# Second attention of a four-layer graph network: the threshold search's one-column chains moved from VectorE to GpSimd and rewritten

## The chip, the core and the metric

The kernel runs on one core of a Trainium2 chip. The metric is device time in microseconds (us) of one execution. Four compute engines work side by side, each through its own queue strictly in order: TensorE (PE in the profile, its weight loads PEld), VectorE (DVE), ScalarE (ACT) and GpSimd (POOL). SyncE (SP) starts the DMAs here. An instruction whose input comes from another engine waits at the head of its queue on a semaphore, and all that is queued behind it on that engine waits too. Measurements of this kernel agree within about 0.2%.

## The reference

Four graph layers work one after another on 3327 nodes with 256 features; each ends in `x = layernorm(x + layer(x, adj))`. The change touches the second of the two attention steps of the last layer:

```python
def _top_p_attention(X, W1, W2, W3):
    q = X @ W1.T @ W2.T
    k = X @ W3.T
    probs = softmax(q @ k.T / TAU)             # 3327 x 3327
    idx = argsort(-probs); sp = probs in that order; cs = cumsum(sp)
    keep_sorted = cs - sp < TOP_P              # TOP_P = 0.9
    A = probs * mask                           # the largest that hold 90% of the mass
    return A / max(A.sum(-1), 1e-12)

R = row-normalized (S + I); Xf = Xa = X; Z = 0
for n in range(2):
    A = _top_p_attention(Xa, W1, W2, W3)
    Xf = R @ Xf
    Xa = A @ Xa
    Z = Z + Xf @ U1[n].T + Xa @ U2[n].T
h = X + Z
return (h - mean) / sqrt(var + eps) * ln_g + ln_b
```

The hard part is the mask: for each row, the probability at which the sorted mass passes 0.9. The kernel doesn't sort; it searches for the threshold.

## The kernel before, in words

Rows are padded to 26 tiles of 128; a row of scores `e` is 128x3328 per tile and is cut in two halves of 1664 columns. The second attention is the last stage, from about 2650 us to the end of the span at 3517.5 us. One trip of its outer loop works on four tiles at once, at different steps, and the steps are interleaved by hand: generators are advanced by `next(...)` in a fixed sequence (`search(i)`, `slot(...)`, `next(result)`), and `here = tc.keep_in_program_order` pins the large instructions of PE and ACT to it. DVE and POOL instructions that are not pinned are ordered by the framework's scheduler. One trip holds:

- **Scores** (`scores`, L1038 on PE, copied to `e` by ACT in L1022): four chunks of the row for the tile two ahead. GpSimd fills one padding column (L1029).
- **Search** (`search_long`), which is what the change rewrites. (a) ACT makes two exponentials of the row: L1169 with half the exponent, whose row sum is `root`, and L1171, whose row sum is `total`. From these a first threshold `c1 = 0.301 (total/root)^2` is made on DVE (L1176 to L1182), and `lim = -0.9 total` on POOL (L1174). (b) ACT measures the row at `c1` with a Relu (L1184, sum `f1`) and a Sign (L1186, sum `sg`); from the count and mass above it, DVE makes a second threshold `c2` in one chain of one-column instructions (L1188 to L1204), while POOL makes the side values `big`, `s` and `ends` (L1207 to L1214). (c) ACT measures again at `c2` (L1216 Relu, L1218 Sign), and DVE makes the third threshold `c3` (L1220 to L1230). (d) DVE takes what lies below `c3` in both halves (`z`, L1236: a scalar_tensor_tensor whose two tensor inputs are both the row in SBUF), finds the eight largest of each 128 columns (13 MAX8 a half, L1103), ranks them (L1114, L1116), finds the crossing (L1123 to L1126), works out ties (L1251 to L1260), drops ties (two match_replace, L1266), and masks the whole row in place (L1274, a scalar_tensor_tensor with both inputs in SBUF, 128x3328).
- **Diffusion** (`diffused`): POOL makes `t` (L1068, L1072), PE sums 26 products (L1058), DVE adds (L1077).
- **Attention values** (`attended`): PE transposes the masked row four blocks at a time (`tp`, L1087), ACT copies each group out of PSUM (`wt`, L1089 through the wrapper in L1022), PE multiplies (L1091). Groups of copies lie in ACT's pinned order between the search's seven row-wide instructions.
- **Result** (`second`): DVE adds (L1318) and takes statistics (L88, L89). POOL adds the bias (L1320), makes `1/sqrt(var)` (`power`: L821 an add, L822 a power, both 128x1), normalizes (L1326 a tensor_scalar, L1327 and L1328 tensor_tensors, all 128x256), and after a second pair of statistics again L821, L822 and L1336. ACT writes the final normalization (L1337).

A chain step for one tile is one instruction on 128x1: one number per row. So the search consists of a few large instructions, and between them DVE and POOL chains whose cost is not data but instruction time.

Two lines order things explicitly: `bound[0]` is the last instruction of chain (b), and each match_replace is issued behind the newest one (`with tc.issue_after(bound[0].ins)`).

Of the kernel before, what the change touches and what calls it, by code (L numbers as in the profile page):

```python
# [9 lines left out]
F32 = mybir.dt.float32  # L10
# [3 lines left out]
ALU = mybir.AluOpType  # L14
# [33 lines left out]
def gnn_kernel(ctx: ExitStack, tc: tile.TileContext, n: int, a: dict, out: bass.AP):  # L48
# [763 lines left out]
    with tc.tile_pool(name="l3", bufs=1) as pool, tc.tile_pool(name="l3d", bufs=1, space=DRAM) as dram:  # L812
# [184 lines left out]
        sd = dram.tile([nt, P, D], F32, name="sd")  # L997
        u1, u2 = (load(pool, x) for x in ("U1", "U2"))
        g3, b3 = (load_row(pool, x) for x in ("ln3_g", "ln3_b"))
        factors = pool.tile([P, 4], F32, name="factors")  # L1000
        for k, x in enumerate((-0.5, -1.0, 0.3, 1.5)):
            nc.vector.memset(factors[:, k:k + 1], x)
        ones = pool.tile([P, 8 * max(RP0, RPT)], F32, name="ones")
        nc.vector.memset(ones, 1.0)
# [144 lines left out]
            yield  # L1149

        junks = [None]
        bound = [None]

        def search_long(work, sm, e, total, v, kept, halves=False):

            def t(name):  # L1160
                return t1(sm, name)

            m8, neg, root = t1(sm, "m8", 8), t1(sm, "neg", 2), t("root")
            nc.vector.max(m8, e[:, :KC])
            nc.gpsimd.tensor_scalar(neg, factors[:, :2], m8[:, 0:1], None, op0=ALU.mult)

            junk = junks[0] = junks[0] or work.tile([P, npad], BF16, name="junk", bufs=1)
            yield
            here(nc.scalar.activation(junk, e, AF.Exp, bias=neg[:, 0:1], scale=0.5, accum_out=root))  # L1169
            yield  # L1170
            here(nc.scalar.activation(e, e, AF.Exp, bias=neg[:, 1:2], accum_out=total))  # L1171
            yield
            lim = t("lim")
            nc.gpsimd.tensor_scalar(lim, total, -TOP_P, None, op0=ALU.mult)  # L1174
            c1 = t("c1")
            nc.vector.reciprocal(c1, root)  # L1176
            nc.vector.tensor_mul(c1, c1, total)
            nc.vector.scalar_tensor_tensor(c1, c1, 0.301, c1, op0=ALU.mult, op1=ALU.mult)


            nc1, f1, sg, k1, m1 = t("nc1"), t("fs1"), t("sg"), t("k1"), t("m1")
            nc.vector.tensor_scalar_mul(nc1, c1, -1.0)  # L1182
            yield
            here(nc.scalar.activation(junk, e, AF.Relu, bias=nc1, accum_out=f1))  # L1184
            yield
            here(nc.scalar.activation(junk, e, AF.Sign, bias=c1, scale=-1.0, accum_out=sg))  # L1186
            yield
            nc.vector.tensor_scalar(k1, sg, -0.5, npad / 2, op0=ALU.mult, op1=ALU.add)  # L1188
            nc.vector.scalar_tensor_tensor(m1, k1, c1, f1, op0=ALU.mult, op1=ALU.add)
            rc, na = t("rc"), t("na")  # L1190
            nc.vector.reciprocal(rc, c1)
            nc.vector.tensor_scalar(na, m1, lim, rc, op0=ALU.add, op1=ALU.mult)

            den, nu, p, q = t("den"), t("nu"), t("p"), t("q")
            nc.vector.tensor_scalar(den, k1, 0.5, UNDER, op0=ALU.mult, op1=ALU.add)
            nc.vector.reciprocal(den, den)
            nc.vector.tensor_scalar(nu, na, UNDER, den, op0=ALU.add, op1=ALU.mult)
            nc.vector.tensor_scalar(p, nu, 0.0, 1.0, op0=ALU.max, op1=ALU.add)
            nc.vector.tensor_sub(q, p, nu)
            nc.vector.reciprocal(q, q)  # L1200
            c2 = t("c2")
            nc.vector.scalar_tensor_tensor(c2, p, c1, q, op0=ALU.mult, op1=ALU.mult)
            nc2, f2, k2, m2 = t("nc2"), t("fs2"), t("k2"), t("m2")
            bound[0] = nc.vector.tensor_scalar_mul(nc2, c2, -1.0)  # L1204

            big = t("big")
            nc.gpsimd.tensor_tensor(big, k1, na, op=ALU.subtract)  # L1207
            nc.gpsimd.tensor_scalar(big, big, 32.0, HUGE, op0=ALU.is_lt, op1=ALU.mult)

            s, dm, ends, same = t("s"), t("dm"), t1(sm, "ends", 2), t("same")  # L1210
            nc.gpsimd.tensor_tensor(s, c2, c1, op=ALU.subtract)
            nc.gpsimd.tensor_scalar(same, s, 0.0, None, op0=ALU.is_equal)
            nc.gpsimd.tensor_tensor(s, s, same, op=ALU.add)
            nc.gpsimd.tensor_scalar(ends, factors[:, 2:], k1, 1.0, op0=ALU.mult, op1=ALU.max)  # L1214
            yield
            here(nc.scalar.activation(junk, e, AF.Relu, bias=nc2, accum_out=f2))  # L1216
            yield
            here(nc.scalar.activation(junk, e, AF.Sign, bias=c2, scale=-1.0, accum_out=sg))  # L1218
            yield
            nc.vector.tensor_scalar(k2, sg, -0.5, npad / 2, op0=ALU.mult, op1=ALU.add)  # L1220
            nc.vector.scalar_tensor_tensor(m2, k2, c2, f2, op0=ALU.mult, op1=ALU.add)
            nc.vector.reciprocal(s, s)
            nc.vector.tensor_sub(dm, m1, m2)
            nc.vector.tensor_mul(s, s, dm)
            nc.vector.tensor_scalar(s, s, ends[:, 0:1], ends[:, 1:2], op0=ALU.max, op1=ALU.min)
            nc.vector.reciprocal(s, s)
            c3 = t("c3")
            nc.vector.scalar_tensor_tensor(c3, c2, UNDER, m2, op0=ALU.mult, op1=ALU.add)
            nc.vector.tensor_scalar(c3, c3, lim, s, op0=ALU.add, op1=ALU.mult)
            nc.vector.scalar_tensor_tensor(c3, c3, c2, big, op0=ALU.add, op1=ALU.max)  # L1230
            rest, base = t("rest"), t("base")
            cand = candidates(work)
            for h, r in enumerate((rest, base)):
                part = e[:, h * half:(h + 1) * half]
                z = work.tile([P, half], F32, name="z", bufs=1)
                x = nc.vector.scalar_tensor_tensor(z, part, c3, part, op0=ALU.is_lt, op1=ALU.mult, accum_out=r)  # L1236
                if h:
                    here(x)
                yield
                segment_tops(cand[:, h * half // SEG * 8:], z, half // SEG)  # L1240
                yield

            nc.gpsimd.tensor_scalar(base, base, rest, total, op0=ALU.add, op1=ALU.subtract)
            nc.gpsimd.tensor_scalar(rest, big, 1.0, base, op0=ALU.is_lt, op1=ALU.mult)
            base = rest
            top = ranked(work, cand, RPT)
            cs = crossing(work, v, top, base, lim, ALU.subtract, ALU.is_le)
            yield
# [12 lines left out]
            sums = t1(sm, "sums", 2)  # L1261
            for i, c in enumerate((0, half)):
                drop = drops[:, i, :]
                part = e[:, c:c + half]
                with tc.issue_after(bound[0].ins):
                    nc.vector.match_replace(part[:, ::-1], drop, part[:, ::-1], 0.0)  # L1266
                if halves:
                    nc.vector.scalar_tensor_tensor(part, part, v, part, op0=ALU.is_ge, op1=ALU.mult,
                                                   accum_out=sums[:, i:i + 1])
            yield  # L1270
            if halves:
                nc.vector.tensor_add(kept, sums[:, :1], sums[:, 1:])
            else:
                nc.vector.scalar_tensor_tensor(e, e, v, e, op0=ALU.is_ge, op1=ALU.mult, accum_out=kept)  # L1274
            yield
# [39 lines left out]
        def second(work, psum, it, acc, f, xf):  # L1315
# [5 lines left out]
            mv = small.tile([P, 2], F32, name="mv")  # L1321
            stats(mv, h)
            rs = small.tile([P, 1], F32, name="rs")
            power(rs, mv)
            yield
            nc.gpsimd.tensor_scalar(h, h, mv[:, 0:1], rs, op0=ALU.subtract, op1=ALU.mult)  # L1326
            nc.gpsimd.tensor_tensor(h, h, g3, op=ALU.mult)  # L1327
            nc.gpsimd.tensor_tensor(h, h, xb, op=ALU.add)  # L1328
            yield
# [40 lines left out]
        with tc.tile_pool(name="l3w", bufs=2) as work, tc.tile_pool(name="l3s", bufs=4) as sm, \  # L1370
# [41 lines left out]
            with tc.tile_pool(name="l3q", bufs=3, space=PSUM) as psum:  # L1412
                es, searches, xfs = {}, {}, []
                result = iter(())
                for i in range(-2, nt + 1):
# [52 lines left out]
                    if 0 < i:  # L1468
                        f = normalizer(sm, kepts[1][:, i - 1:i], tots[1][:, i - 1:i])
                        result = second(work, psum, i - 1, next(values), f, xfs[i - 1])  # L1470
                both(result)
                fl = unresolved(sm, psum, 1)

            fi0 = pool.tile([1, nt + 1], I32, name="fi0")
# [140 lines left out]
```

## Time and profile before

| what | value |
|---|---|
| median of 3 runs | 3516.83 us (3515.82 to 3521.38) |
| the profiled execution | 3519.38 us, its span 3517.5 us (1.9 us lie around it) |
| busy over the span | PE 92%, DVE 67%, ACT 49%, POOL 27% |
| second attention, 2750 to 3430 us (680 us) | PE 662.45, DVE 652.24, ACT 570.31, POOL 247.57 us busy |
| start of L1326, from 2876.58 to 3402.72 us | 17 trips, 30.95 us each |
| L1327 on POOL in that stage | 0.72 us at least, 2.25 us in the median |

How to read it: the shares over the span are averages over four layers with different limits, so only the rows of the second attention count here. A "group" is a set of instructions of one line, engine and shape with its count, its sum of busy time, the mean of one and the idle time just before. A timeline row has the start and the duration in us, the engine, the line, what is written from what, and in brackets the idle time before it with the instruction that ended it. PE's end times are modelled.

### The profile page before, as it was taken

What the parts mean: (1) busy time and instruction counts of PE and PEld (TensorE: products, weight loads), DVE (VectorE), ACT (ScalarE), POOL (GpSimd) and SP (SyncE); (2) the same over time, 40 slices, a digit from 0 to 9 for tenths busy, and PEclk for the clock granted to TensorE, in tenths of its full rate; (3) what the DMA queues carried; (4) which work ended last, traced back from release to release, by engine and by line L of the source; (5) the groups of instructions that cost most, each with busy time, mean ns of one, the idle gap of its engine ahead of it and who ended that gap; (6) DMA issues with size and microseconds to landing.
All of it is one profiled execution on the core that took longest, in us unless ns stands there. A gap on an engine that the chain in (4) does not pass through costs nothing. (4 is left out here: it accounts for less than half of the span.)

```text
span 3517.5 us, 43266 instructions
## 1 busy us (share of the span) xinstructions
PE 3235.5 (92%) x15597; PEld 2540.3 (72%) x15597; DVE 2370.4 (67%) x5245; ACT 1740.6 (49%) x2751; POOL 932.8 (27%) x942
## 2 busy tenths in 40 slices
PE   9999988988888766999899999999997999999996
PEld 7888766676676555888677878787775777777775
DVE  1111177999999997777454544444434999999996
ACT  0000356767667675111133333333336888888883
POOL 0000054666665653121100000000001243333332
PEclk9999998999999888999899999999999999999998
DMA  7443334334443222344321212121212112222220
GB/s 248 139 140 110 102 109 112 101 119 106 106 119 91 66 58 92 126 140 145 95 66 56 65 49 65 48 67 47 67 47 74 55 56 67 68 70 61 70 65 16
DMA packets 147577, 307.99 MB, mean 88 GB/s; under 512 B 19570, under 2 KB 68850, under 8 KB 147218
## 3 DMA queue, kind: packets, MB, share of 16 engines
q1 hardware_dynamic: 147346, 305.06, 29.7%
q8 instruction: 126, 2.06, 0.2%
q14 instruction: 105, 0.86, 0.1%
HBM read 294.36 MB, written 10.65 MB: 87 GB/s over the span
## 5 line engine op out<-in xcount | busy, mean ns | idle before, releaser
L274 POOL TENSOR_TENSOR h<-du,row 128x2048 f32<-128x2048 f32 (+1 forms) x110 | 465.7, 4233 | 339.3 <-DVE hc L274 270.8
L274 DVE TENSOR_TENSOR_SCAN h<-dA,carry,h 128x512 f32<-128x512 f32 (+1 forms) x384 | 448.7, 1220 | 19.8 <-ACT dA L281 19.7
L281 ACT ACTIVATE dA<-t,A_log 128x512 f32<-128x512 f32 (+1 forms) x448 | 292.3, 658 | 146.4 <-DVE h L274 143.4
L1058 PE MATMUL acc<-F,at 128*128 128x256 f32 x1352 | 353.5, 387 | 1.0 <-ACT q L832 0.6
L1091 PE MATMUL acc<-X,wt 128*128 128x256 f32 x1352 | 343.5, 390 | 10.5 <-ACT wt L1089 10.2
L1091 PE MATMUL acc<-G,wt 128*128 128x256 f32 x1352 | 336.8, 392 | 6.4 <-ACT wt L1022 5.9
L1091 PEld LDWEIGHTS acc<-X,wt 128*128 128x128 f32 x1352 | 242.6, 189 | 105.3 <-issue 41.3
L120 PE MATMUL acc<-xa,at 128*128 128x257 f32 x1352 | 308.6, 382 | 5.6 <-DMA at<-in_adjT 5.6
L1058 PE MATMUL acc<-X,at 128*128 128x256 f32 x1352 | 308.4, 381 | 0.0
L967 PE MATMUL acc<-F,at 128*128 128x257 f32 x1352 | 303.6, 381 | 1.2 <-DMA U<-in_U 1.2
L333 PE MATMUL cb<-F,at 128*128 128x256 f32 x1196 | 294.0, 394 | 7.4 <-ACT hn L353 4.5
L1091 PEld LDWEIGHTS acc<-G,wt 128*128 128x128 f32 x1352 | 250.1, 193 | 67.0 <-ACT wt L1022 36.8
L1103 DVE MAX8 cand<-e 128x8 f32<-128x128 f32 x676 | 142.2, 278 | 229.0 <-ACT e L1044 217.4
L1058 PEld LDWEIGHTS acc<-F,at 128*128 128x128 f32 x1352 | 237.9, 190 | 75.3 <-issue 50.2
L120 PEld LDWEIGHTS acc<-xa,at 128*128 128x128 f32 x1352 | 255.7, 191 | 42.4 <-issue 5.5
L1058 PEld LDWEIGHTS acc<-X,at 128*128 128x128 f32 x1352 | 252.9, 191 | 40.2 <-issue 7.0
L967 PEld LDWEIGHTS acc<-F,at 128*128 128x128 f32 x1352 | 253.4, 190 | 36.8 <-issue 1.4
L333 PEld LDWEIGHTS cb<-F,at 128*128 128x128 f32 x1196 | 228.8, 197 | 59.4 <-issue 14.3
L624 PE MATMUL y<-ident,hc 128*128 128x128 f32 x1664 | 229.7, 291 | 42.9 <-DVE hc L274 42.3
L624 PEld LDWEIGHTS y<-ident,hc 128*128 128x128 f32 x1664 | 204.5, 151 | 82.5 <-DVE hc L274 59.3
L274 DVE TENSOR_TENSOR hc<-h,row 128x2048 f32<-128x2048 f32 (+2 forms) x114 | 242.8, 2131 | 11.0 <-PE y L624 4.3
L1089 ACT COPY wt<-tp 128x512 f32<-128x512 f32 (+1 forms) x182 | 93.5, 557 | 309.2 <-PE tp L1087 309.0
(352 smaller groups left out, 5264.1 us busy)
## 6 DMA issues: line engine op xcount, KB each, us to landing
at<-in_adjT SPq DMA_DIRECT2D x102, 832.0 KB, 4.6
at<-in_adjT SPq DMA_DIRECT2D x260, 320.0 KB, 2.9
row<-bc SPq DMA_DIRECT2D x80, 512.0 KB, 5.1
at<-in_adjT SPq DMA_DIRECT2D x52, 576.0 KB, 4.0
at<-in_adjT SPq DMA_DIRECT2D x26, 512.0 KB, 3.8
row<-bc SPq DMA_DIRECT2D x32, 384.0 KB, 5.0
xt<-in_xT SPq DMA_DIRECT2D x26, 128.0 KB, 4.1
qd<-q SPq DMA_DIRECT2D x104, 32.0 KB, 1.9
```

Source lines behind the costliest of these rows:

```text
L120: nc.tensor.matmul(acc, at[:, j, :], rhs[:, j0 + j, :], start=(j0 + j == 0), stop=(j0 + j == nt - 1))
L274: return lambda *x, **k: tc.keep_in_program_order(op(*x, **k))
L281: decays.append(op(*x, **k))
L333: ten.matmul(acc, at[:, j % JC, :], X0[:, j, :], start=(j == 0), stop=(j == nt - 1))
L624: x = ten.matmul(y[:, g * P:(g + 1) * P], h[:, g, i * P:(i + 1) * P], ident, is_transpose=True, start=(first and g == 0), stop=(last and g ...
L967: nc.tensor.matmul(acc, at[:, j, :], F[:, j0 + j, :], start=(j0 + j == 0), stop=(j0 + j == nt - 1))
L1058: nc.tensor.matmul(acc, at[:, j, :], rhs[:, j0 + j, :], start=(j0 + j == 0), stop=(j0 + j == nt - 1))
L1089: copy(wt[:, :m, :], pt[:, :m, :])
L1091: nc.tensor.matmul(acc, wt[:, j, :], rhs[:, j0 + j, :], start=(j0 + j == 0), stop=(j0 + j == nt - 1))
L1103: nc.vector.max(cand[:, s * 8:(s + 1) * 8], z[:, s * SEG:(s + 1) * SEG])
```

## The change

Three things are changed, all in the second attention.

1. The chains that make `c1`, `c2` and `c3` are put on GpSimd as a whole. Reciprocals become powers with exponent -1, and two columns are worked at once where `c` and `-c` are wanted. `root^-2` and its products with 0.301 and -0.301 (`squares`) are made behind the first exponential, so that only one instruction (`c1s`) lies between `total` and the Relu at `c1`. The update of `c2` is written with fewer quotients.
2. The wait of match_replace on `bound` is dropped.
3. In `second`, the first `power` and the first normalization (the old L1326) are issued behind the newest `c3` instruction (`edge`), on GpSimd's queue.

```diff
-        factors = pool.tile([P, 4], F32, name="factors")
-        for k, x in enumerate((-0.5, -1.0, 0.3, 1.5)):
+        factors = pool.tile([P, 8], F32, name="factors")
+        for k, x in enumerate((-0.5, -1.0, 0.3, 1.5, 0.301, -0.301, -2.0, -1.0)):
...
-        bound = [None]
+        edge = [None]
+
+        def behind_edge():
+            return tc.issue_after(edge[0].ins) if edge[0] is not None else nullcontext()
...
             here(nc.scalar.activation(junk, e, AF.Exp, bias=neg[:, 0:1], scale=0.5, accum_out=root))
             yield
+            squares = t1(sm, "squares", 2)
+            nc.gpsimd.tensor_tensor(root, root, factors[:, 6:7], op=ALU.pow)
+            nc.gpsimd.tensor_scalar(squares, factors[:, 4:6], root, None, op0=ALU.mult)
             here(nc.scalar.activation(e, e, AF.Exp, bias=neg[:, 1:2], accum_out=total))
             yield
-            lim = t("lim")
-            nc.gpsimd.tensor_scalar(lim, total, -TOP_P, None, op0=ALU.mult)
-            c1 = t("c1")
-            nc.vector.reciprocal(c1, root)
-            nc.vector.tensor_mul(c1, c1, total)
-            nc.vector.scalar_tensor_tensor(c1, c1, 0.301, c1, op0=ALU.mult, op1=ALU.mult)
-            nc1, f1, sg, k1, m1 = t("nc1"), t("fs1"), t("sg"), t("k1"), t("m1")
-            nc.vector.tensor_scalar_mul(nc1, c1, -1.0)
+            gps = nc.gpsimd
+            def scaled(dst, x, a, b, op0, op1):
+                return gps.tensor_scalar(dst, x, a, b, op0=op0, op1=op1)
+            def raised(x, k):
+                gps.tensor_tensor(x, x, factors[:, k:k + 1], op=ALU.pow)
+            c1s, lim, rc = t1(sm, "c1", 2), t("lim"), t("rc")
+            scaled(c1s, squares, total, total, ALU.mult, ALU.mult)
+            c1, nc1 = c1s[:, 0:1], c1s[:, 1:2]
+            gps.tensor_scalar(lim, total, -TOP_P, None, op0=ALU.mult)
+            gps.tensor_tensor(rc, c1, factors[:, 7:8], op=ALU.pow)
...
             here(nc.scalar.activation(junk, e, AF.Sign, bias=c1, scale=-1.0, accum_out=sg))
             yield
-            nc.vector.tensor_scalar(k1, sg, -0.5, npad / 2, op0=ALU.mult, op1=ALU.add)
...
-            bound[0] = nc.vector.tensor_scalar_mul(nc2, c2, -1.0)
...
+            scaled(k1, sg, -0.5, npad / 2, ALU.mult, ALU.add)
+            scaled(m1, k1, c1, f1, ALU.mult, ALU.add)
+            na, more, room, less = t("na"), t("more"), t("room"), t("less")
+            scaled(na, m1, lim, rc, ALU.add, ALU.mult)
+            scaled(room, k1, 0.5, UNDER, ALU.mult, ALU.add)
+            scaled(more, na, UNDER, 0.0, ALU.add, ALU.max)
+            gps.tensor_tensor(more, more, room, op=ALU.add)
+            scaled(less, more, na, UNDER, ALU.subtract, ALU.subtract)
+            raised(less, 7)
+            c2, nc2, f2, k2, m2 = t("c2"), t("nc2"), t("fs2"), t("k2"), t("m2")
+            scaled(c2, more, less, c1, ALU.mult, ALU.mult)
+            gps.tensor_scalar(nc2, c2, -1.0, None, op0=ALU.mult)
+            yield
+            here(nc.scalar.activation(junk, e, AF.Relu, bias=nc2, accum_out=f2))
...
+            gps.tensor_tensor(s, c1, c2, op=ALU.subtract)
+            gps.tensor_scalar(same, s, 0.0, None, op0=ALU.is_equal)
+            gps.tensor_tensor(s, s, same, op=ALU.add)
+            raised(s, 7)
+            scaled(ends, factors[:, 2:4], k1, 1.0, ALU.mult, ALU.max)
             here(nc.scalar.activation(junk, e, AF.Sign, bias=c2, scale=-1.0, accum_out=sg))
             yield
-            nc.vector.tensor_scalar(k2, sg, -0.5, npad / 2, op0=ALU.mult, op1=ALU.add)
...
-            nc.vector.scalar_tensor_tensor(c3, c3, c2, big, op0=ALU.add, op1=ALU.max)
+            scaled(k2, sg, -0.5, npad / 2, ALU.mult, ALU.add)
+            scaled(m2, k2, c2, f2, ALU.mult, ALU.add)
+            scaled(s, m2, m1, s, ALU.subtract, ALU.mult)
+            scaled(s, s, ends[:, 0:1], ends[:, 1:2], ALU.max, ALU.min)
+            raised(s, 7)
+            c3 = t("c3")
+            scaled(c3, c2, UNDER, m2, ALU.mult, ALU.add)
+            scaled(c3, c3, lim, s, ALU.add, ALU.mult)
+            edge[0] = scaled(c3, c3, c2, big, ALU.add, ALU.max)
...
-                with tc.issue_after(bound[0].ins):
-                    nc.vector.match_replace(part[:, ::-1], drop, part[:, ::-1], 0.0)
+                nc.vector.match_replace(part[:, ::-1], drop, part[:, ::-1], 0.0)
...
-            power(rs, mv)
-            yield
-            nc.gpsimd.tensor_scalar(h, h, mv[:, 0:1], rs, op0=ALU.subtract, op1=ALU.mult)
+            with behind_edge():
+                power(rs, mv)
+            yield
+            with behind_edge():
+                nc.gpsimd.tensor_scalar(h, h, mv[:, 0:1], rs, op0=ALU.subtract, op1=ALU.mult)
```

In the order of instructions that the changed kernel is built to, the queues of PE and ACT are the same as before in the full trips. GpSimd's queue holds in one full trip, after the change and in this order: the eight instructions of chain (c) up to `c3`; `power` (2), the normalization (3), `t` (L1068, L1072), `neg`; `c1s`, `lim`, `rc`; `base`, `rest`; `power` (2) and the last scale; the thirteen of chain (b) up to `-c2`, with `big` and `ends` among them; four for `s`; `root` and `squares`; the padding column; the bias addition. 22 trips have this full sequence. On DVE, the two `z`, the row mask, the ranking and the statistics keep their places, and the chains' instructions between them are gone.

More of the change, by code (lines that the diff above doesn't have):

```diff
@@ L1170, in search_long @@
             yield
+            squares = t1(sm, "squares", 2)
+            nc.gpsimd.tensor_tensor(root, root, factors[:, 6:7], op=ALU.pow)
+            nc.gpsimd.tensor_scalar(squares, factors[:, 4:6], root, None, op0=ALU.mult)
             here(nc.scalar.activation(e, e, AF.Exp, bias=neg[:, 1:2], accum_out=total))
             yield
-            lim = t("lim")
-            nc.gpsimd.tensor_scalar(lim, total, -TOP_P, None, op0=ALU.mult)
-            c1 = t("c1")
-            nc.vector.reciprocal(c1, root)
-            nc.vector.tensor_mul(c1, c1, total)
-            nc.vector.scalar_tensor_tensor(c1, c1, 0.301, c1, op0=ALU.mult, op1=ALU.mult)
-            nc1, f1, sg, k1, m1 = t("nc1"), t("fs1"), t("sg"), t("k1"), t("m1")
-            nc.vector.tensor_scalar_mul(nc1, c1, -1.0)
+            gps = nc.gpsimd
[8 more added lines that the diff above has]
+            gps.tensor_tensor(rc, c1, factors[:, 7:8], op=ALU.pow)
+            f1, sg, k1, m1 = t("fs1"), t("sg"), t("k1"), t("m1")
             yield
@@ L1187, in search_long @@
             yield
-            nc.vector.tensor_scalar(k1, sg, -0.5, npad / 2, op0=ALU.mult, op1=ALU.add)
[L1189 to L1203, printed above, removed]
-            bound[0] = nc.vector.tensor_scalar_mul(nc2, c2, -1.0)
[L1206 to L1214, printed above, removed]
+            scaled(k1, sg, -0.5, npad / 2, ALU.mult, ALU.add)
[10 more added lines that the diff above has]
+            gps.tensor_scalar(nc2, c2, -1.0, None, op0=ALU.mult)
             yield
@@ L1217, in search_long @@
             yield
+            big = t("big")
+            gps.tensor_tensor(big, k1, na, op=ALU.subtract)
+            scaled(big, big, 32.0, HUGE, ALU.is_lt, ALU.mult)
+            s, same, ends = t("s"), t("same"), t1(sm, "ends", 2)
+            gps.tensor_tensor(s, c1, c2, op=ALU.subtract)
[3 more added lines that the diff above has]
+            scaled(ends, factors[:, 2:4], k1, 1.0, ALU.mult, ALU.max)
             here(nc.scalar.activation(junk, e, AF.Sign, bias=c2, scale=-1.0, accum_out=sg))
             yield
-            nc.vector.tensor_scalar(k2, sg, -0.5, npad / 2, op0=ALU.mult, op1=ALU.add)
[L1221 to L1226, printed above, removed]
+            scaled(k2, sg, -0.5, npad / 2, ALU.mult, ALU.add)
[3 more added lines that the diff above has]
+            raised(s, 7)
             c3 = t("c3")
-            nc.vector.scalar_tensor_tensor(c3, c2, UNDER, m2, op0=ALU.mult, op1=ALU.add)
-            nc.vector.tensor_scalar(c3, c3, lim, s, op0=ALU.add, op1=ALU.mult)
-            nc.vector.scalar_tensor_tensor(c3, c3, c2, big, op0=ALU.add, op1=ALU.max)
+            scaled(c3, c2, UNDER, m2, ALU.mult, ALU.add)
+            scaled(c3, c3, lim, s, ALU.add, ALU.mult)
+            edge[0] = scaled(c3, c3, c2, big, ALU.add, ALU.max)
             rest, base = t("rest"), t("base")
@@ L1471, in gnn_kernel @@
                 both(result)
+                edge[0] = None
                 fl = unresolved(sm, psum, 1)
```

## The prediction

> **What bounds the kernel now.** I read the table by stretches of 100 us first, because the shares over the span mix four layers. Its columns are PE, PEld, DVE, ACT, POOL (busy us, instructions), the granted clock, the DMA share and GB/s:
>
> ```profile
> 2900.00:3000.00 100.00, 99.38 (x477) 73.78 (x477) 95.93 (x314) 85.70 (x83) 34.87 (x70) 1.00 0.23 68
> ```
>
> PE and DVE are both nearly full; DVE's missing 4% are gaps of some 60 ns between instructions. Which one ends the trip is told by the timeline of one trip. First ACT and PE, then POOL and DVE:
>
> ```profile
> 3008.26 3.07 ACT L1184 ACTIVATE junk<-e,nc 128x3328 bf16<-128x3328 f32 x1
> 3015.86 0.19 ACT L1186 ACTIVATION_READ_ACCUMULATOR junk<-e,c 128x1 f32 x1
> 3021.70 3.07 ACT L1216 ACTIVATE junk<-e,nc 128x3328 bf16<-128x3328 f32 x1
> 3028.21 0.19 ACT L1218 ACTIVATION_READ_ACCUMULATOR junk<-e,c 128x1 f32 x1
> 3039.09 3.07 ACT L1184 ACTIVATE junk<-e,nc 128x3328 bf16<-128x3328 f32 x1
> 3028.61 0.63 PE L1087 MATMUL tp<-ident,e 128*128 128x128 f32 x4 [0.43 <-DVE e L1274]
> ```
> ```profile
> 3001.41 1.95 DVE L1236 SCALAR_TENSOR_TENSOR z<-e,c 128x1664 f32<-128x1664 f32 x1
> 3024.78 3.67 DVE L1274 SCALAR_TENSOR_TENSOR e<-e,v 128x3328 f32<-128x3328 f32 x1
> 3000.36 1.25 POOL L1326 TENSOR_SCALAR h<-h,mv,rs 128x256 f32<-128x256 f32 x1
> 3001.70 2.25 POOL L1327 TENSOR_TENSOR h<-h,ln_g 128x256 f32<-128x256 f32 x1
> 3006.60 0.29 POOL L1165 TENSOR_SCALAR neg<-factors,m 128x2 f32<-128x2 f32 x1
> ```
>
> The reader is to see that PE waits once a trip, 0.43 us, for DVE's row mask: DVE ends the trip (30.95 us), and PE would need 30.95 - 0.43 = 30.5. ACT goes in lockstep: 10.7 us from the end of the second Sign (3028.40) to the next first Relu (3039.09), 7.8 from there to the end of the first Sign (3008.26 to 3016.05), 13.4 to the second Relu (3021.70), and 6.7 from that to the end of the second Sign. 10.7 + 13.4 + 6.7 is the trip.
>
> The last view is what an instruction on POOL costs when DVE works on two SBUF tensors at the same time:
>
> ```profile
> 2870.64 3.68 DVE L1274 SCALAR_TENSOR_TENSOR e<-e,v 128x3328 f32<-128x3328 f32 x1
> 2870.80 4.10 POOL L1320 TENSOR_TENSOR t<-X,ln_b 128x256 f32<-128x256 f32 x1 [3.51 <-DVE xf L1077]
> 1423.45 1.87 DVE L964 SCALAR_TENSOR_TENSOR at<-at,w 128x1664 f32<-128x1664 f32 x1
> 1423.61 1.78 POOL L821 TENSOR_SCALAR rs<-mv 128x1 f32<-128x1 f32 x1 [33.38 <-DVE mv L89]
> 1425.36 1.89 DVE L961 TENSOR_TENSOR w<-r,q 128x1664 f32<-128x1664 f32 x1
> 1425.48 2.19 POOL L822 TENSOR_TENSOR rs<-rs,mhalf 128x1 f32<-128x1 f32 x1
> 2696.64 1.95 DVE L1236 SCALAR_TENSOR_TENSOR z<-e,c 128x1664 f32<-128x1664 f32 x1
> 2698.22 0.46 POOL L1174 TENSOR_SCALAR lim<-tot 128x1 f32<-128x1 f32 x1 [1.84 <-ACT e L1171]
> ```
>
> L1320 takes 0.73 elsewhere, L821 0.22, L822 0.57, L1174 0.21. Each of these ends just after the DVE instruction, one-column ones too: POOL **stands still** while DVE reads two SBUF tensors. Beside MAX8 or match_replace it doesn't. In a trip DVE does this for 1.95 + 1.94 + 3.67 = 7.6 us: two `z` and the mask.
>
> **The change, part by part.** *DVE.* From the timeline, by start to next start, leave: the chain to `-c2` 1.96 us (3018.97 to 3020.93), the chain to `c3` 1.74, the one to `-c1` 1.04, three reciprocals 0.2: 4.9 us, so some 26 of 30.95 stay. Alone, this would make PE the bound: 0.43 x 22 full trips = 9.5 us gained.
>
> *Dropping `bound`* costs and gains nothing: match_replace lies behind its own data (the drops) on the same queue.
>
> *POOL's instructions.* Rows: 0.24 with two constants (L1208), 0.30 with a column and a constant (L1244), 0.38 with two columns (L1243), 0.59 a power, 0.19 a tensor_tensor; about 0.1 more where one needs the result just before (L821's end to L822's start). A power with exponent -1 or -2 isn't in the trace, only one with -0.5. I bound it by 0.19 (any other 128x1 tensor_tensor) and by twice 0.59 and take 0.59, as it is the same instruction; the ends move (b) and (c) by -0.4 and +0.6 each. POOL goes from 11 us a trip to some 23, held time included: it isn't full. What counts is when each chain ends. Take t = 0 at the end of the second Sign.
>
> *(c), up to `c3`:* 0.24 + 5 x 0.38 + 0.30 + 0.59 + 6 waits x 0.1, and 0.1 to begin: **3.7 us**. (Now 4.0, most of it DVE's queue.) The first `z` runs from 3.75 to 5.7.
>
> *Ordering the result behind it.* `power` now begins at 3.7: its add (0.22) slips through, its power meets `z` and ends at 6.2 instead of 4.6. L1326's work 6.3 to 7.6; the two tensor_tensors of 0.73 (free, DVE is in MAX8) 7.7 to 9.3, over DVE's wish to start the second `z` at 8.8, which is held until 9.3, as L1072 (0.74) now holds DVE's L1177 (0.70 instead of 0.16) in each trip. `z` runs 9.3 to 11.2; `t` (0.93) is held behind it and ends at 12.05; L1072's work 12.9; `neg` 13.2; `c1s` (two columns, 0.43) **13.6**. The Relu that wants it would start at 10.7, so ACT stands 2.9 us, and PE with it: the next copy of `wt` lies behind this Relu. Now L1165 ends at 3006.9, before ACT needs it, as the normalization begins earlier.
>
> *(b), up to `-c2`:* the first Sign ends 7.8 later, at 21.4. 13 instructions: 3 x 0.38 + 4 x 0.24 + 0.35 + 0.30 + 2 x 0.19 + 0.59 + 0.21 = 3.9, with 9 waits **4.8 us**, to 26.2. But DVE's mask begins at 25.1: second `z` to 11.2, MAX8s 2.5, statistics 0.3, ranking to drops 7.1, two match_replace with their waits 3.9. So the last two or three, from the power or `c2` on, stand until 28.7, and `-c2` comes at 29.4. The second Relu would have been ready at 13.6 + 13.4 = 27.0: 2.4 us more.
>
> *Trip:* 29.4 + 6.7 = **36.1 us**, against 30.95: 5.2 more, in 22 trips 114 us. Here the large terms are robust: they are `z`, the mask and the DVE work between, all from rows. By 20% on POOL's short rows the trip moves by about 1 us. No DMA is added; the result's writes to DRAM follow ACT's L1337 and move with it, and no one waits for them within the trip.
>
> *Edges.* In the first trips there is no result. The first `c2` comes 1.6 us late (4.8 us on POOL behind a Sign, while ACT is busy for only 3.2 us with the next tile's exponential, which now covers DVE's 2 us), the first `c3` 3 us (1.6, and 3.7 instead of 2.3 for the chain), the next ones meet the mask of the tile before: 7 us by my estimate, between 0 and 12. At the end the last `z` comes some 2 us late, and the tail has no chain on its path: 2 us.
>
> *Sum:* 3519.4 (profiled) + 114 + 7 + 2 = 3642; the median before lies 2.6 lower, so **3640**.
>
> The Trainium skill ("SBUF — State Buffer", Who interferes with whom) states this as a rule: whoever issues first gets the shared ports for the whole instruction, and the other one blocks. The rows agree where DVE is first or POOL has a tensor_tensor; they differ for POOL's tensor_scalar, since L1326 at 3000.36 overlaps `z` at 3001.41, which takes its usual 1.95. By the rule a power on POOL could also hold the mask by up to 0.59, 13 us over 22 trips.
>
> **Rivals.** *A: only the first hold.* If (b) gets through before the mask (it needs 0.9 us: shorter POOL instructions, or `t` not held as I think), the trip is 13.6 + 13.4 + 6.7 = 33.7, 2.8 more: 3516.8 + 62 + 7 = 3586. Against it: both POOL's chain and the mask's start are near, but 0.9 us is five short instructions.
>
> *B: faster.* If POOL isn't held by `z` in this order, `c1s` comes at 3.7 + 0.3 + 0.7 + 1.35 + 2 x 0.83 + 1.75 + 0.3 + 0.45 = 10.2, before 10.7; (b) takes 18.5 to 23.3, before the mask at 24.6; PE bounds at 30.5: 9.5 us, and 0 to 6 in the first trips, where PE waits 2 us for the mask in three of them; I take 2.5: 3505. For it: DVE is relieved where it is the bound. It decides from the point where `c1s` takes under 11 us; against it stand the four held rows.
>
> *C: worse.* After PE waits of over 2 us its next work can be slow: behind 2.27 us (2872.20) six matmuls L1058 took 2.50 instead of 1.46. If ACT meets this in each trip it costs about 1 us: 3662.
>
> *D: no change.* (b) escapes and `c1s` comes near 11: 3517.
>
> **Chances.** Forecast 0.56, A 0.14, C 0.10, between A and D 0.05, D 0.04, B 0.11. Within 0.2% (3509.8 to 3523.9) can't be told from no change. Faster 0.11, same 0.04, slower 0.85. The range takes the forecast, A and C with their edges (±12): 3570 to 3670, which leaves out 0.2.
>
> **What would show it.** After: starts of the old L1326 some 36 us apart; ACT's first Relu waiting about 3 us for POOL's `c1s`, the second about 2.4 for `-c2`; a `c2`-chain instruction of over 3 us that ends with the mask; the power behind `c3` over 2 us, `t` over 2.5; the h-by-g tensor_tensor down from 2.25 to 0.73; DVE at some 26 of 36 us. A trip under 31 us, or short rows beside the mask, would prove me wrong.

## The result, and the profile after

The changed kernel takes 3624.01 us (median of 4 runs, 3619.46 to 3626.29) against 3519.11 (4 runs on the same chip): ratio 1.0292, 95% interval 1.0278 to 1.0305. It is **slower by 2.9%**; the forecast was 3640 in a range of 3570 to 3670. The profiled execution has a span of 3622.6 us against 3517.5.

Over the span PE has 3263.2 us, DVE 2282.0 (88 less than before) and POOL 1250.3 (318 more). The stretch of the second attention that was shown of before, with the same columns:

```profile
2900.00:3000.00 100.00, 88.39 (x416) 65.03 (x414) 75.57 (x213) 72.38 (x71) 66.94 (x127) 0.98 0.20 58
```

DVE fell from 95.93 to 75.57, as meant, but PE fell from 99.38 to 88.39, and POOL went from 34.87 to 66.94. No engine is full any more: the trip is ended by waits. The timeline of one steady trip tells which. It begins with the end of a second Sign at 3105.44 (t = 0) and ends with the last ACT row, t = 35.36:

```profile
3108.68 0.38 POOL L1182 TENSOR_SCALAR c<-c,c,big 128x1 f32<-128x1 f32 x1
3109.15 1.98 POOL L821 TENSOR_SCALAR rs<-mv 128x1 f32<-128x1 f32 x1
3113.20 0.72 POOL L1332 TENSOR_TENSOR h<-h,ln_g 128x256 f32<-128x256 f32 x1
3114.83 2.44 POOL L1068 TENSOR_SCALAR t<-F,rdeg 128x256 f32<-128x256 f32 x1
3118.36 0.33 POOL L1182 TENSOR_SCALAR c<-squares,tot 128x2 f32<-128x2 f32 x1
3130.60 3.69 POOL L1210 TENSOR_SCALAR nc<-c 128x1 f32<-128x1 f32 x1
3109.10 1.95 DVE L1240 SCALAR_TENSOR_TENSOR z<-e,c 128x1664 f32<-128x1664 f32 x1 [4.34 <-POOL c L1182]
3114.11 2.36 DVE L1240 SCALAR_TENSOR_TENSOR z<-e,c 128x1664 f32<-128x1664 f32 x1
3130.51 3.69 DVE L1277 SCALAR_TENSOR_TENSOR e<-e,v 128x3328 f32<-128x3328 f32 x1
3118.72 3.07 ACT L1194 ACTIVATE junk<-e,c 128x3328 bf16<-128x3328 f32 x1 [2.74 <-POOL c L1182]
3134.32 3.07 ACT L1212 ACTIVATE junk<-e,nc 128x3328 bf16<-128x3328 f32 x1 [2.35 <-POOL nc L1210]
3140.61 0.19 ACT L1224 ACTIVATION_READ_ACCUMULATOR junk<-e,c 128x1 f32 x1
```

Line 5 is `c1s`, line 6 is `-c2`; the brackets at the end of a row are the idle time of its engine and who ended it. Three POOL rows are far over their usual length (0.22, 0.93 and 0.23). L821 and L1210 end within 0.1 us of the first `z` and of the mask; L1068 ends 0.8 us after the second `z`, nearly its own length later. L1210 begins 0.09 us after the mask and lasts as long as it. ACT stands 2.74 and 2.35 us for the two results. The old 2.25 us of the h-by-g tensor_tensor (now L1332) are 0.72: the stall moved, it did not go.

Where the 105.1 us of the span lie, counted from the ends of the second Sign: 0.9 before the first, 21.6 in the first seven trips (233.3 against 211.7), 76.6 in the next seventeen (601.2 against 524.6), 5.9 after that.

### The profile page after: what moved, and what is told of

Same layout as the page of the kernel before. It is cut to its first block, busy times and chain, and to the rows that moved or that the text cites. A ratio compares the mean times of both kernels' runs of the same rounds, so it can differ in the third digit from the quotient of the medians.

```text
span 3622.6 us, 43190 instructions
## 1 busy us (share of the span) xinstructions
PE 3263.2 (90%) x15597; PEld 2552.3 (70%) x15597; DVE 2282.0 (63%) x4573; ACT 1739.4 (48%) x2751; POOL 1250.3 (35%) x1540
## 5 line engine op out<-in xcount | busy, mean ns | idle before, releaser
L1091 PE MATMUL acc<-G,wt 128*128 128x256 f32 x1352 | 348.9, 402 | 90.2 <-ACT wt L1022 89.3
L967 PEld LDWEIGHTS acc<-F,at 128*128 128x128 f32 x1352 | 253.4, 190 | 36.8 <-issue 1.4
```

The costliest lines, as they stand in the source:

```text
L967: nc.tensor.matmul(acc, at[:, j, :], F[:, j0 + j, :], start=(j0 + j == 0), stop=(j0 + j == nt - 1))
L1091: nc.tensor.matmul(acc, wt[:, j, :], rhs[:, j0 + j, :], start=(j0 + j == 0), stop=(j0 + j == nt - 1))
```

## The experiments

All are judged by the ratio to the kernel before (95% interval) and by the trips in their traces. "First 7" and "next 17" are sums over trips from one second Sign's end to the next, in the one profiled execution of each kernel; "steady trip" is the usual length among the seventeen.

| kernel | ratio | first 7 | next 17 | steady trip |
|---|---|---|---|---|
| before | 1 | 211.7 | 524.6 | 30.59 to 31.23 |
| after | 1.0292 [1.0278, 1.0305] | 233.3 | 601.2 | 35.37 |
| e1, without the order | 1.0348 [1.033, 1.0365] | 251.3 | 594.1 | 34.92 |
| e2, mask waits for -c2 | 1.021 [1.0193, 1.0227] | 223.0 | 579.9 | 33.14, or 34.71 to 34.84 |
| e3, `t` late | 1.0084 [1.0067, 1.0101] | 228.6 | 534.2 | 31.42 |
| e5, DVE reads one SBUF tensor | 1.0054 [1.0037, 1.0071] | 228.4 | 520.0 | 30.59 |
| e6, chain (a) on DVE | 1.005 [1.0033, 1.0067] | 226.9 | 522.0 | 30.69 |
| e7, `c1s` first | 1.0021 [1.0011, 1.0031] | 220.9 | 520.0 | 30.59 |
| e8, e7 with the mask's wait | 1.0025 [1.0015, 1.0034] | 221.3 | 520.1 | 30.59 |
| e9, first 8 tiles old | 0.9983 [0.9974, 0.9992] | 212.0 | 520.0 | 30.59 |
| e10, first 4 tiles old | 0.9998 [0.9987, 1.0009] | 208.6 | 520.0 | 30.59 |
| e11, e5 without the order | 1.040, a single run | 263.0 | 596.6 | 33.4 to 36.8 |

### e4: who is held, by itself

Each pair runs alone, released by one copy on ACT:

```diff
+        here(nc.scalar.copy(b, go))
+        here(GPS.memset(go, 0.25))
...
+        here(DVE.memset(b, 0.25))
+        dve(d, z, r, m8)                      # 128x1664: two SBUF inputs / second in PSUM / one input / MAX8
+        here(GPS.memset(pad[:, :lead], 0.0))
+        pool_op(q, x, hh)                     # five kinds; in other cases POOL's goes ahead of DVE's
```

> Only a measurement: the whole network is left out, and pairs of instructions are run side by side, each pair alone. DVE: a 128x1664 select with both inputs in SBUF, the same with the second input in PSUM, the same with one input, and MAX8. POOL: one column times a constant, one column with two pointers, a power of one column, tensor_scalar and tensor_tensor of 128x256, issued after DVE's began; then the other way round, with DVE's select begun 0.1 to 1 us after a POOL instruction. Holds: beside the select with two SBUF inputs every POOL instruction that begins in it ends with it (up to 1.95 us), and beside the other three none is longer than alone (0.23, 0.38, 0.57, 1.25, 0.73). DVE's select is held by POOL's tensor_tensor for as long as that runs, but not by a tensor_scalar that began over 0.1 us earlier. Rival, any big DVE instruction slows POOL: all four columns alike. Rival, one-column instructions slip through: only the 128x256 ones are held.

The timeline, POOL first, then the DVE instruction beside some of them:

```profile
6.14 1.82 POOL L82 TENSOR_SCALAR x_two_imm<-c 128x1 f32<-128x1 f32 x1
11.52 2.11 POOL L86 TENSOR_TENSOR x_two_pow<-c,k 128x1 f32<-128x1 f32 x1
20.91 0.23 POOL L82 TENSOR_SCALAR x_psum_imm<-c 128x1 f32<-128x1 f32 x1
33.35 0.23 POOL L82 TENSOR_SCALAR x_one_imm<-c 128x1 f32<-128x1 f32 x1
73.54 3.18 POOL L88 TENSOR_SCALAR y_ts_first_m<-h,c 128x256 f32<-128x256 f32 x1
77.31 0.72 POOL L90 TENSOR_TENSOR y_tt_first_a<-h,g 128x256 f32<-128x256 f32 x1
5.93 1.95 DVE L71 SCALAR_TENSOR_TENSOR z<-e,b 128x1664 f32<-128x1664 f32 x1
20.64 1.95 DVE L73 SCALAR_TENSOR_TENSOR z<-e,b,pcol 128x1664 f32<-128x1664 f32 x1
74.20 1.83 DVE L71 SCALAR_TENSOR_TENSOR z<-e,b 128x1664 f32<-128x1664 f32 x1
77.30 2.49 DVE L71 SCALAR_TENSOR_TENSOR z<-e,b 128x1664 f32<-128x1664 f32 x1
```

The same one-column instruction takes 1.82 us beside a select with two SBUF inputs and 0.23 beside the same select with its second input in PSUM (`pcol`) or beside a comparison with a single input, though DVE is busy for 1.95 us in all three. The other three kinds of DVE work left all five POOL kinds at their own time. So it is the second SBUF input that holds a POOL instruction which begins in the select, whatever POOL's size. The last part of my expectation fell: a POOL tensor_scalar that began 0.66 us ahead of the select (73.54 against 74.20) was held all the same and ended 0.69 after it, while a 128x256 tensor_tensor that was issued first held the select (2.49). A one-column power that was issued first did neither: begun between 0.41 us before the select and 0.02 after its start, it took 0.55 to 0.57 us, and the select 1.83 to 1.95.

### e1: the change without its order

```diff
-            with behind_edge():
+            if True:
                 power(rs, mv)
...
-            with behind_edge():
+            if True:
                 nc.gpsimd.tensor_scalar(h, h, mv[:, 0:1], rs, op0=ALU.subtract, op1=ALU.mult)
```

> The change without its order: the result's normalization and power are no longer queued behind c3 on POOL. In the recorded order of POOL they then stand ahead of the chain to c3, and the diffused product's `t` stands in the middle of it. Holds (my forecast's theory): t = 0 is the end of the second Sign. The row's statistics are ready at -0.7, so the normalization ends at 3.8, `c3` comes at 8.8 instead of 3.6, `c1s` at 11.3 instead of 13.1, the second `z` ends at 15.4 and the mask begins near 29.4, long after -c2 (23.5): neither hold is left on the path, but the mask ends 2.5 us into the next trip and PE waits for it there. Trip 31 to 32 us instead of 35.4, sum 3624 - 21 x 3.9 = 3540 (3520 to 3560). Rival, POOL's chains are simply slow and the holds cost little: c3 comes 5 us later, so the trip grows to 37 to 40 us, 3660 to 3720. Rival, the order is the whole cost: 3517 to 3524.

3642.8 us, 18.8 more than with the order; no theory had this. The loss lies at the ends: the first seven trips take 18.0 us more than with the order and what follows the seventeen 7.5 more, while the steady trip, 34.92, is 0.45 us shorter than with the order, though far from the 31 to 32 expected. I had taken the statistics of the result as ready at t = -0.7, as they are in the changed kernel. Without the order `c3` comes late, so `z`, the mask and the next statistics come late too, which delays the next `c3`: a ring that I had not closed. e11 tests the new reading.

### e11: the same, with nothing on POOL held

```diff
-                x = nc.vector.scalar_tensor_tensor(z, part, c3, part, op0=ALU.is_lt, op1=ALU.mult, accum_out=r)
+                x = nc.vector.tensor_scalar(z, part, c3, 0.0, op0=ALU.is_lt, op1=ALU.add, accum_out=r)
...
-                nc.vector.scalar_tensor_tensor(e, e, v, e, op0=ALU.is_ge, op1=ALU.mult, accum_out=kept)
+                nc.vector.tensor_scalar(e, e, v, 0.0, op0=ALU.is_ge, op1=ALU.add, accum_out=kept); nc.vector.tensor_scalar(kept, total, TOP_P, None, op0=ALU.mult)
```

(and the edit of e1)

> The change without its order, and with DVE's selects and mask reading one SBUF tensor (the selected values and the true kept sum are left out, as in the run with one input), so that nothing on POOL is held. The run without the order failed my reckoning (trip 31 to 32 us, measured 34.9). New theory: without the order POOL does the normalization and `t` ahead of the end of the chain to c3, which closes a ring that needs no hold: statistics of the result to `c3` 8.7 us on POOL, `c3` to the next statistics 26.2 us on DVE, 34.9 together. Then the trip stays at 34.9 to 35.0 with no hold at all, where the same kernel with the order took 30.6. Rival, the holds make that trip long too (a `c1s` held by `z` is seen in it): 31 to 33.

A single run, 3660 us. The trips are 33.4 to 36.8 us and 35.1 in the mean, with no POOL instruction over 1.3 us. The mean is close to what was expected; what spreads the trips is not shown. The ring in the timeline of one trip, from the statistics to the next ones:

```profile
3100.62 0.18 DVE L89 BATCH_NORM_AGGREGATE mv<-bnst 128x2 f32<-128x6 f32 x1
3109.15 0.38 POOL L1182 TENSOR_SCALAR c<-c,c,big 128x1 f32<-128x1 f32 x1
3109.56 1.95 DVE L1240 TENSOR_SCALAR_CACHE_REDUCE z<-e,c 128x1664 f32<-128x1664 f32 x1 [8.28 <-POOL c L1182]
3135.72 0.18 DVE L89 BATCH_NORM_AGGREGATE mv<-bnst 128x2 f32<-128x6 f32 x1
```

8.9 us from the statistics to `z` through POOL, 26.2 from `z` to the next statistics through DVE: 35.1, the mean trip. With the order and without holds (e5) it is 30.59: where nothing is held, the order is worth 4.5 us a trip. With the holds in place it makes the steady trip 0.45 us longer (35.37 against 34.92 in e1), and what it saves lies in the first trips and at the end.

### e2: the mask waits for -c2

```diff
-            gps.tensor_scalar(nc2, c2, -1.0, None, op0=ALU.mult)
+            gps.tensor_scalar(nc2, c2, -1.0, None, op0=ALU.mult); bound[0] = nc.vector.tensor_copy(t("seen"), nc2)
...
+                with tc.issue_after(bound[0].ins):
                     nc.vector.scalar_tensor_tensor(e, e, v, e, op0=ALU.is_ge, op1=ALU.mult, accum_out=kept)
```

> A wait is added and nothing taken away: a tiny copy of the newest -c2 on DVE, and the row mask is queued behind it, so that the mask can't begin before POOL's chain (b) has ended. Holds: -c2 comes at 25.2 after the second Sign instead of 28.8, the mask begins 0.3 us later than now, and every trip becomes like the two of the changed kernel in which -c2 escaped (31.9 us): 3624 - 20 x 3.45 = 3555 (3545 to 3570). First hold alone is left. Rival, POOL's chains are simply slower: a wait more on DVE can't help, 3624 to 3634.

3596.1 us: a wait more and 28 us less than the changed kernel, but 41 above my number. -c2 did escape in every steady trip, and the first hold stayed (Relu at 13.3). Two things were missed. The two trips of 31.9 us that I took as the price had drawn on a lead of PE; without that lead ACT waits 0.27 and 0.76 us a trip for transposed blocks, 1.0 of the 1.2 us up to 33.14. And in ten of the seventeen trips PE comes back slowly from its wait of 2.36 us. The matmuls behind that wait in a trip of 34.83 and in one of 33.14, and stretches of 2 us from the same two trips, with the granted clock behind POOL's column:

```profile
3074.54 3.62 PE L1091 MATMUL acc<-G,wt 128*128 128x256 f32 x8 [2.36 <-ACT wt L1022]
3109.37 1.99 PE L1091 MATMUL acc<-G,wt 128*128 128x256 f32 x8 [2.36 <-ACT wt L1022]
```
```profile
3074.00:3076.00 2.00, 1.46 (x4) 1.19 (x5) 1.76 (x7) 2.00 (x3) 0.00 (x0) 0.69 0.00 0
3076.00:3078.00 2.00, 2.00 (x7) 1.55 (x6) 1.79 (x12) 2.00 (x3) 0.26 (x2) 0.50 0.00 0
...
3109.00:3111.00 2.00, 1.63 (x8) 1.45 (x9) 1.76 (x6) 2.00 (x2) 0.00 (x0) 1.00 0.00 0
```

The eight matmuls behind the wait take 3.62 us at a clock of 0.50 to 0.69 and 1.99 at 1.00: 1.63 of the 1.69 us between the two kinds of trip.

### e3: `t` behind `c1s`

```diff
             for acc in aggregated(atp, psum, it, Y if p else X, each):
                 if acc is None: yield
+            if p:
+                with (tc.issue_after(guess[0].ins) if guess[0] is not None else nullcontext()):
+                    nc.gpsimd.tensor_scalar(t, Y[:, it, :], rd, None, op0=ALU.mult); nc.gpsimd.tensor_tensor(t, t, s, op=ALU.add)
...
+            guess[0] = scaled(c1s, squares, total, total, ALU.mult, ALU.mult)
```

> Only POOL's queue is changed: the diffused product's `t` (two instructions of 128x256, needed at the end of the trip) is issued behind `c1s` instead of ahead of it. Holds: `c1s` is held by the second `z` alone, until 11.0 after the second Sign, and comes at 11.2 instead of 13.1; -c2 follows 12.1 later, at 23.4, before the mask begins (25.1), so the second hold goes too without being touched. Trip 30.5 (PE's own) to 31 us; 3624 - 21 x 4.6 = 3527 (3512 to 3540). Rival, the second wait has its own cause (chain b is 4.8 us long on POOL): only the first 1.9 us are saved, 3624 - 21 x 1.9 = 3584 (3575 to 3595). Rival, POOL isn't held by `z` but was late by its own work: `c1s` at 10.5, 3510 to 3520.

3552.3 us, steady trip 31.42. `neg` now meets `z` in place of `t`, but ends with it, and the first Relu starts at 11.58. The second hold vanished untouched, as my theory said. The last rival would have had it gone as well, but by it POOL isn't held by `z`, and here `neg` is, for 1.95 us:

```profile
3058.36 1.95 POOL L1168 TENSOR_SCALAR neg<-factors,m 128x2 f32<-128x2 f32 x1
3060.31 0.34 POOL L1182 TENSOR_SCALAR c<-squares,tot 128x2 f32<-128x2 f32 x1
3072.61 0.24 POOL L1210 TENSOR_SCALAR nc<-c 128x1 f32<-128x1 f32 x1
```

L1210 takes 0.24 instead of 3.69. Moving two instructions in a queue saved 1.7 us of the first wait and 2.3 of the second. The sum missed the upper end by 12 us: trips 2, 3 and 5 took 35.8, 38.5 and 37.9 us.

### e5: no holds

The edit of e11, with the change's order kept.

> The changed kernel, with its POOL chains and its order untouched, but DVE's two selects and its mask read one SBUF tensor instead of two: a comparison with a column and a constant add, whose 1664-element row took the same 1.95 us beside POOL without holding it (measured by itself). What is left out: the selected values (ones stand in their place) and the true kept sum (0.9 of the total stands there), so the result isn't the reference's; instructions, sizes, order and waits stay, plus one tiny DVE instruction a trip. Holds: with no instruction on POOL held, `c1s` comes before ACT asks for it (10.5 after the second Sign), -c2 at 23, and PE alone ends the trip: 30.5 us, 3505 to 3525, at or below the kernel before. Rival, POOL's chains are simply longer than DVE's were: nothing changes, 3600 to 3630. In between would mean that both count.

3537.9 us. The steady trip is PE's 30.59, and the stretch is full again:

```profile
2900.00:3000.00 100.00, 99.44 (x480) 73.89 (x479) 86.27 (x259) 83.19 (x82) 58.46 (x148) 1.00 0.22 67
```

Same chains, same order, same queues, and 86 of the 105 us are gone: the holds, and not the chains' length, make the steady trip long. The first seven trips still lose 16.7 us against the kernel before; the next seventeen gain 4.5. In the first four, PE waits 31.4 us for the mask instead of 16.3, and the first `z` starts 3.7 us after the second Sign instead of 2.3; how much of that loss is the chains' length and how much their order is not shown.

### e6: chain (a) back on DVE

```diff
-            nc.gpsimd.tensor_tensor(root, root, factors[:, 6:7], op=ALU.pow)
-            nc.gpsimd.tensor_scalar(squares, factors[:, 4:6], root, None, op0=ALU.mult)
...
-            scaled(c1s, squares, total, total, ALU.mult, ALU.mult)
+            nc.vector.reciprocal(c1, root); nc.vector.tensor_mul(c1, c1, total)
+            nc.vector.scalar_tensor_tensor(c1, c1, 0.301, c1, op0=ALU.mult, op1=ALU.mult); nc.vector.tensor_scalar_mul(nc1, c1, -1.0)
```

> One part of the change undone: the chain that ends in c1 and -c1 is back on DVE (four one-column instructions), the two others and the order stay on POOL. Holds: DVE makes -c1 before the second `z`, near 9 us after the second Sign, so the first Relu starts at its own time, 10.5; -c2 follows 12.3 later, near 23, before the mask at 26 (DVE has 1 us more to do), so the second hold goes too. Trip 30.5 to 31 us: 3624 - 21 x 4.6 = 3527 (3515 to 3545). Rival, each of the three chains costs its own part: only the first wait (2.7 us) goes and the second stays, trip 33, 3570 to 3580.

3535.6 us, trip 30.69: inside the range. `t` still takes 2.68 us in every trip (0.93 when it isn't held), and it costs nothing, since no one waits for it. A hold is only a price where the held result is wanted.

### e7 and e8: `c1s` first, then the mask's wait on top

```diff
-            with behind_edge():
+            with (tc.issue_after(guess[0].ins) if guess[0] is not None else nullcontext()):
                 nc.gpsimd.tensor_scalar(h, h, mv[:, 0:1], rs, op0=ALU.subtract, op1=ALU.mult)
```

(on top of e3; e8 adds e2's edit and applies e3's `issue_after` only to tiles with `it > 3`)

> As the run with `t` late, and the result's normalization (not its power) is queued behind `c1s` instead of behind `c3`. Holds: `c1s` now stands right behind the power and comes near 7 us after the second Sign, clear of both `z`; the first Relu starts at 10.5, 1.1 earlier than with `t` late, and the trip falls from 31.4 to PE's 30.5: 3552 - 21 x 0.9 = 3533 (3525 to 3545), the early trips unchanged. The normalization is held by the second `z` instead, which costs nothing if it ends before DVE's second statistics (13.5). Rival, PE already bounds at 31.4: 3548 to 3556.

> As the run before it, with the diffused product's `t` left free in the first four tiles, and the mask made to wait for the newest -c2. In the steady trip neither does anything (-c2 comes 2 us before the mask), so this is for the first trips: with `t` late they took 35.8, 38.5, 30.2 and 37.9 us instead of some 31, because the mask fell on a chain of POOL. Holds: the guard takes the mask away from chain (b), not from chain (c): 10 of those 20 us are saved, 3522 (3510 to 3535). Rival, the early trips are slow for another reason (their first use of each buffer, DMA): as the run before it within 4 us.

e7: 3526.8 us, steady trip 30.59, within the range; the first seven trips, which I had expected unchanged, take 7.7 us less than in e3. e8: 3528.6, no better, as its rival said. Its first six trips are other ones (29.0, 33.2, 33.7, 32.0, 30.8 and 32.9 instead of 24.9, 35.6, 35.0, 30.1, 34.7 and 30.9) with nearly the same sum, so my reading that the mask's meeting with the chains makes them slow fell; e5, where nothing is held, has 228.4 there.

### e9 and e10: the first tiles in the old form

```diff
+            if old:                           # old: t < 8 (e9), t < 4 (e10)
+                here(nc.scalar.activation(e, e, AF.Exp, bias=neg[:, 1:2], accum_out=total))
...
+            else:
                 squares = t1(sm, "squares", 2)
```

(on top of e7; the old branch is the code of before, and as long as it runs, so do its order of `t` and of the normalization)

> A version meant to beat both: the first eight tiles of the second attention keep the chains on DVE as in the kernel before, all later ones have them on POOL, with `c1s` ahead of the result's normalization and of `t`. Theory: what is left of the loss in the run with c1 first lies in the first seven trips (220.9 us against 211.7 before), where PE has no backlog and waits out POOL's longer chains, and then runs at half the granted clock for some us; the later trips are at PE's 30.59 and take 520.0 instead of 524.6. With both good parts: 3520 - 4.6 = 3515 to 3516 (3512 to 3520). Rival, the early trips are lost to the other order of the queues and not to the chains: 3523 to 3528, as before this edit. Rival, the seam between the two forms costs a trip: 3518 to 3524.

> The same with only the first four tiles' chains on DVE. If the loss comes from the first trips while PE has no backlog (trips 2 and 3), this gives the same 3515 to 3518; if every trip up to the seventh is short of backlog, trips 4 to 6 lose again, some 3 to 6 us, 3518 to 3522.

e9: 3515.38 against 3520.85 us, 0.9983 [0.9974, 0.9992]: **below both kernels**, clear of 1 but by only 0.17% against the kernel before. Its two parts are the sums foreseen, 212.0 and 520.0. e10's profiled execution (3515.24 us) has 208.6 and 520.0, yet its runs spread from 3511.96 to 3529.05 and its ratio can't be told from 1, so which number of old tiles is best stays open. Stretches of 5 us in the first trips, e7 and then e9:

```profile
2725.00:2730.00 5.00, 5.00 (x16) 3.75 (x14) 2.66 (x5) 3.64 (x3) 2.01 (x6) 0.50 0.00 0
2750.00:2755.00 5.00, 1.59 (x6) 1.53 (x7) 3.59 (x4) 5.00 (x4) 4.70 (x4) 0.57 0.00 0
```
```profile
2725.00:2730.00 5.00, 5.00 (x26) 3.42 (x24) 4.93 (x21) 1.34 (x2) 0.70 (x3) 0.94 0.00 0
2750.00:2755.00 5.00, 4.96 (x30) 3.47 (x28) 4.75 (x17) 5.00 (x7) 3.99 (x4) 1.00 0.23 66
```

With the chains on POOL, PE (first pair of numbers) stands for most of the second stretch and works at half the clock in both; in the old form it is full, and the clock is back. Since e9 gives back the old chains and the old order of those tiles together, the runs don't tell how much each of them is worth there.

## Why the prediction was right, point by point

- **What bounds the kernel** (PE at 30.5 behind DVE at 30.95): right. Without holds the trip is 30.59 (e5, e7). But the kernel before already had four of the seventeen trips at 30.59, so relieving DVE is worth 4.5 us in the seventeen, where I had taken 9.5 for 22.
- **POOL stands still beside two SBUF inputs of DVE**: right, shown alone by e4 and in place by e5.
- **`c3` at 3.7, power until 6.2, normalization over the second `z` until 9.3, `t` until 12.05, `c1s` at 13.6**: measured 3.6, 6.3, 9.3, 11.8 and 13.25; the first Relu starts at 13.3. One detail was other: it is `power`'s add that `z` holds (1.98 us), and its power runs freely behind it (0.55); that the end came out the same, 6.3, is luck. So the sign "the power over 2 us" did not show as written, and `t` took 2.44 where I had asked for over 2.5.
- **Chain (b) meets the mask, -c2 at 29.4**: measured 28.85. Only -c2 itself was caught, where I had two or three instructions behind the mask. For rival A I had asked 0.9 us of margin; 0.3 decides: in two trips the mask began at 25.36 instead of 25.07, after `-c2` had begun (25.17), `-c2` kept its 0.23 us, and the trip took 31.9.
- **Trip 36.1**: measured 35.37. The 0.7 are 0.3 at `c1s`, 0.2 more up to the second Relu, and 0.2 behind it.
- **Dropping `bound`**: no run has it by itself. In the timeline after, match_replace begins 0.04 us after its drops are made (3126.66 after 3126.62), so nothing else delays it there.
- **The term that was most mis-sized: the 22 full trips.** The sum was 17.9 too high in the span (123 against 105.1), and 16.2 of it are these trips: 97.8 us, forecast 114. Less came by the smaller steady trip and by the two trips of 31.9; more by one trip of 40.2, in which DVE's queue waited 8.4 us for PE's sum, and because the 22 trips of the kernel before took 30.83 us in the mean where I had used 30.95. The edges were further off for their size, 1.5 in the part before the 22 (forecast 7) and 5.9 at the end (2); that their sum, 7.4, is near the forecast 9 is luck.
- **Rivals.** A's trip of 33.7 lies between the 33.14 and the 34.83 of e2 (34.1 in the mean), and e2 as a whole at 3596.1 where I had 3586. B's mechanism, POOL not held, is e5: the steady trip came as I wrote it, but the whole at 3537.9 instead of 3505, most of all since the first trips lose 16.7 us even then, where I had booked a gain of 2.5. C, PE slow behind its waits: the granted clock did fall in 13 of the changed kernel's seventeen steady trips (0.95 to 0.98 in the mean of a trip, 1.00 in the other four), but all seventeen took 35.36 or 35.37, so it cost nothing there; in e2 it cost 1.69 us in ten trips.

The Trainium skill ("SBUF — State Buffer", Who interferes with whom) says that a DVE instruction with at most one SBUF input, outside the two-port modes, does not contend with GpSimd: e4 agrees, with 0.23 us beside it and 1.82 beside two inputs. It also says that the order of issue decides who blocks; e4 agrees for a 128x256 tensor_tensor (2.49 us for the select behind it) and not for a tensor_scalar, which was held though it began 0.66 us earlier. Nor did a power on one column, issued first, hold the select (1.83 to 1.95 us), so the 13 us that the prediction priced by that rule have nothing behind them here.

## What to carry to other kernels

Before short chains are moved to GpSimd, lay them on one trip's timeline beside DVE's instructions with two SBUF inputs: a one-column step that begins in one ends only with it (3.69 us instead of 0.23 for `-c2`). If one is late, look first at what stands ahead of it in its own queue: here two instructions put behind `c1s` took 1.7 of the 2.7 us off the first wait and the whole of the second. And close the ring before pricing an order: what comes late in one trip comes late in the next one's inputs.

## What the runs showed of the hardware that was not expected

- A POOL tensor_scalar of 128x256 is held even when it began 0.12 to 0.66 us ahead of DVE's select (2.65 to 3.18 us instead of 0.95), and doesn't slow that select (1.83).
- PE's granted clock fell to 0.50 to 0.69 (means over 2 us) behind a wait of 2.36 us in ten of e2's seventeen steady trips and stayed at 1.00 in the others, behind the same wait.
- Powers with exponent -1 and -2 on a column take 0.55 to 0.58 us on POOL, like the one with -0.5.
